# Closer due times for stores, sums and set-up transfers in a planned graph kernel, with four result buffers for six

## The chip, the cores and the metric

The kernel runs on one core of a Trainium2 chip. A core has five engines that matter here: TensorE (PE in the profile, with PEld for its weight loads), VectorE (DVE), ScalarE (ACT), GpSimd (POOL) and SyncE (SP). Each works through its own queue of instructions, and they meet through semaphores. The metric is the device time of one execution in microseconds, as the median of several runs.

## What is computed

Two graph layers over 16 graphs with 1024 nodes of 64 channels each, and a dense adjacency array of 1024 x 1024 per graph that is mostly zeros:

```python
h = jnp.maximum(_layernorm(x, axis=-1), 0.0)
x = x + _L0_gnn_ref(h, adj)          # (adj / clip(row sum, 1)) @ h
h = jnp.maximum(_layernorm(x, axis=-1), 0.0)
x = x + _L1_gnn_ref(h, adj, nodemask, W1, b1, W2, b2)

# in _L1_gnn_ref:
adj_d = _dilate_adj(adj, mask)       # drops some neighbours of nodes with more than 10
agg = _weighted_nanquantile_agg(x, adj_d > 0)   # 0.25*q25 + 0.5*q50 + 0.25*q75, per channel
out = x + agg
h = jax.nn.relu(jnp.einsum('bnc,ch->bnh', out, W1) + b1)
y = jnp.einsum('bnh,ho->bno', h, W2) + b2
```

The second layer takes, for every node and channel, three quantiles over the node's neighbours. Nodes have very different numbers of neighbours, from one to about a hundred.

## The kernel before

**Layer 0.** For each graph, SP loads eight tiles of adjacency rows. TensorE transposes them, ACT copies the transposes out of PSUM, TensorE multiplies them by the normalised features, and VectorE divides by the row sums. ACT and VectorE also make a short list of the neighbours of every node: ACT takes the sign of the row (`sg`), and VectorE picks the largest keys of four segments (`rec`). The streams `loads`, `beginnings`, `signs`, `listing`, `transposes`, `products`, `channels` and `endings` do this, each graph after graph. At the end of a graph, `endings` sorts its nodes by the length of their lists and writes their records to the DRAM table `srt` with eight indirect stores from GpSimd.

**Groups and jobs.** Four graphs form a group. When its four graphs are sorted, `group` (line 1015) reads the records back, gathers one full adjacency row per partition for the longest lists (`gat_rows`), computes which neighbours are dropped, writes marks for two of them into the table of features (`tab`), and starts ten jobs. A job takes T tiles of 128 nodes with lists of equal length. It gathers the neighbours' features with one indirect DMA per list position (`places`), sorts them on VectorE by a network of minima and maxima, weighs them (`prod`), and hands them to `layers` (line 960). There TensorE adds up the terms, transposing them (`pt`), and applies W1 and W2, with ACT between; ACT writes the result `y`; VectorE adds the residual, `y + S`; and GpSimd stores the rows with one indirect DMA per tile (`out_dram`). Four more jobs with the longest lists of all, one tile each, come from `long_lists` (line 1133): their names begin with l (`lat`, `lplaces`). The 44 jobs need 124 stores and 659 gathers.

**The plan.** What sets the order of all this is the class `Plan` (line 233). It runs while the program is built. Every stream is a generator, and each `yield` names the engine that its next step needs and a function for the time at which the step may begin. The plan keeps a clock for each engine and, for each tile, the time at which it is ready, both from fixed costs per operation. Again and again it takes the step that can begin first (of equals, the one with the lower rank), and emits its instructions. On the chip there are no clocks and no due times any more: there is an order of instructions on each engine, and the waits on semaphores that the data need. A step that the plan put too close behind its operand therefore waits at the head of its engine's queue.

Three constants are added to due times for this: `LOOSE` (line 214), 15 us, between a job's last product and TensorE's terms (line 963) and between `y` and the sum (line 1005); `ROWS` (line 215), 7 us, ahead of the sort stores (line 774), of the gather of full rows (`gat_rows`, line 1036, and `lat`, line 1154) and of the marks (line 1110); and `LATE` (line 216), 25 us, between the sum and the stores (line 1010). Since results live long in this way, there are six buffers for `y` (lines 963 and 964). `SLACK`, 2 us, serves in the same way for shorter hand-overs and stays.

Of the kernel before, what the change touches and what calls it, by code (L numbers as in the profile page):

```python
# [9 lines left out]
F32 = mybir.dt.float32  # L10
# [8 lines left out]
P = 128  # L19
# [190 lines left out]
INF = float("inf")  # L210
BREATH = 0.8
AHEAD = 8
SLACK = 2.0
LOOSE = 15.0
ROWS = 7.0
LATE = 25.0


class Timed:
# [13 lines left out]
class Plan:  # L233
# [24 lines left out]
    def room(self, name, bufs):  # L258

        tiles = self.slots.get(name, ())  # L260
        if len(tiles) < bufs:
            return 0.0
        old = tiles[-bufs]
        return INF if self.users[old] else max(self.used.get(old, 0.0), self.ready.get(old, 0.0))

    def at(self, *tiles):
        return max(self.ready.get(t.tensor.name, INF) for t in tiles)
# [98 lines left out]
def list_path(ctx, tc, x, adj, nodemask, w1, b1, w2, b2, out, go):  # L366
# [3 lines left out]
    CO = w2.shape[1]  # L370
# [19 lines left out]
    mlp = ctx.enter_context(tc.tile_pool(name="mlp", bufs=2))  # L390
# [88 lines left out]
    new, free, room, at = plan.tile, plan.release, plan.room, plan.at  # L479
# [235 lines left out]
    def endings(pool, now):  # L715

        for b, st in enumerate(batch):
            now[0] = b
            g, gb = divmod(b, GB)
            yield "ACT", lambda: known(st, "rec", "row") if st["listed"] == NT else INF  # L720
            rec, total, row = st["rec"], st["total"], st["row"]

            for t in range(NT):
                nc.scalar.activation(
                    row[:, t, R0:R0 + 8 * NSEG], rec[:, t, :], AF.Relu, bias=before[:, t:t + 1]
                )


            yield "DVE", always
            found = new(pool, [P, NT, 8 * NSEG], BF, "found", 1)  # L730
            nc.vector.tensor_scalar(found, rec, 0.0, None, op0=OP.is_gt)
            d = new(tiny, [P, NT], F32, "d", 2)
            nc.vector.tensor_reduce(d, found, AX.X, OP.add)
            full = new(tiny, [P, NT], F32, "full", 2)
            nc.vector.tensor_reduce(
                full, found.rearrange("p t (s e) -> p t s e", e=8)[:, :, :, 7], AX.X, OP.max
            )
            nc.vector.scalar_tensor_tensor(d, full, float(STEPS[0]), d, op0=OP.mult, op1=OP.max)
            nc.vector.tensor_scalar(d, d, float(STEPS[0]), None, op0=OP.min)
            for s in STEPS[1:]:  # L740
                nc.vector.scalar_tensor_tensor(d, total, float(s), d, op0=OP.is_gt, op1=OP.add)
            free(rec)
            free(total)
            hot = new(tiny, [P, CLS, NT], BF, "hot", 2)
            nc.vector.tensor_tensor(
                hot, cls, d.unsqueeze(1).to_broadcast([P, CLS, NT]), OP.is_equal
            )
            yield "PE", lambda: max(at(hot), room("ps_small", 3))
            pc = new(ps_s, [P, HALF], F32, "ps_small", 3, users=1)
            K = CLS * NT  # L750
            flat = hot.rearrange("p c t -> p (c t)")
            nc.tensor.matmul(pc[:, :K], earlier, flat, start=True, stop=True)
            nc.tensor.matmul(pc[:, K:2 * K], ones, flat, start=True, stop=True)
            yield "DVE", lambda: at(pc) + SLACK
            base = new(tiny, [P, K], F32, "base", 2)
            nc.vector.tensor_tensor_scan(
                base, pc[:, K:2 * K], zeros[:, :K], 0.0, op0=OP.add, op1=OP.add
            )
            nc.vector.tensor_tensor(base, base, pc[:, K:2 * K], OP.subtract)
            nc.vector.tensor_tensor(base, base, pc[:, :K], OP.add)  # L760
            free(pc)
            nc.vector.tensor_tensor(base, base, flat, OP.mult)
            pos = new(tiny, [P, NT], F32, "pos", 2)
            nc.vector.tensor_reduce(pos, base.rearrange("p (c t) -> p t c", t=NT), AX.X, OP.add)
            low = new(tiny, [P, NT], I32, "low", 2)
            nc.vector.tensor_copy(low, pos)
            nc.vector.tensor_scalar(low, low, LSUB - 1, None, op0=OP.bitwise_and)
            nc.vector.tensor_scalar(
                pos, pos, float(GB), float(LSUB * gb), op0=OP.mult, op1=OP.add
            )  # L770
            to = new(pool, [P, NT], I32, "to", 2)
            nc.vector.scalar_tensor_tensor(to, low, float(1 - GB), pos, op0=OP.mult, op1=OP.add)
            for t in range(NT):
                yield "POOL", lambda: max(at(to), at(row)) + ROWS if "normed" in st else INF
                scatter(srt[g], row[:, t, :], to[:, t:t + 1], sorts[g])
            free(row)
            progress["batches"] = b + 1
# [21 lines left out]
    class Job:  # L799
# [160 lines left out]
        def layers(self, terms, sources):  # L960

            T, R = self.T, terms[0][0].shape[1]
            yield "PE", lambda: max(at(*sources) + LOOSE, room("y", 6), room("pt", 2))
            y = new(mlp, [P, T, CO], F32, "y", 6, users=1)
            for t0 in range(0, T, 4):
                ts = range(t0, min(t0 + 4, T))
                M = len(ts) * P
                if t0:
                    yield "PE", lambda: room("pt", 2)
                pt = new(ps_t, [P, HALF], F32, "pt", 2, users=1)  # L970
                for i, t in enumerate(ts):
                    for k, term in enumerate(terms[t]):
                        nc.tensor.matmul(
                            pt[:term.shape[1], i * P:(i + 1) * P], term, ident,
                            start=(k == 0), stop=(k == len(terms[t]) - 1),
                        )
                if t0 + 4 >= T:
                    for tile_ in sources:
                        free(tile_)
                yield "ACT", lambda: max(at(pt) + SLACK, room("ot", 2))  # L980
                ot = new(mlp, [2 * C, HALF], F32, "ot", 2)
                nc.scalar.copy(ot[:R, :M], pt[:R, :M])
                free(pt)
                yield "PE", lambda: max(at(ot) + SLACK, room("ps_small", 3))
                ph = new(ps_s, [P, HALF], F32, "ps_small", 3, users=1)
                nc.tensor.matmul(ph[:, :M], w1_sb[:R, :], ot[:R, :M], start=True, stop=True)
                yield "ACT", lambda: max(at(ph) + SLACK, room("hid", 2))
                hid = new(mlp, [H, HALF], F32, "hid", 2)
                nc.scalar.activation(hid[:, :M], ph[:, :M], AF.Relu, bias=b1_sb)
                free(ph)  # L990
                yield "PE", lambda: max(at(hid) + SLACK, room("ps_small", 3))
                py = new(ps_s, [P, HALF], F32, "ps_small", 3, users=1)
                pv = py[:, :len(ts) * CO].rearrange("p (t c) -> p t c", c=CO)
                for i, t in enumerate(ts):
                    nc.tensor.matmul(
                        pv[:, i, :], hid[:, i * P:(i + 1) * P], w2_sb, start=True, stop=False
                    )
                    nc.tensor.matmul(pv[:, i, :], ones_f[:1, :], b2_sb, start=False, stop=True)
                yield "ACT", lambda: at(py) + SLACK
                for i, t in enumerate(ts):  # L1000
                    nc.scalar.activation(
                        y[:, t, :], pv[:, i, :], AF.Copy, scale=self.mask[:, t:t + 1]
                    )
                free(py)
            yield "DVE", lambda: at(y) + LOOSE
            nc.vector.tensor_tensor(y, y, self.S[:, :, X1:R0], OP.add)
            if self.short:
                free(self.S)
            for t in range(T):
                yield "POOL", lambda: at(y) + LATE  # L1010
                scatter(out_rows, y[:, t, :], self.nodes_i[:, t:t + 1], scatters)
            free(y)
            progress["jobs"][self.g] += 1

    def group(g):
# [17 lines left out]
        )  # L1033
        nodes_i = new(grp, [P, NTAU], I32, "nodes_i", 2)
        nc.vector.tensor_copy(nodes_i, nodes)
        yield "POOL", lambda: at(nodes_i) + ROWS
        full = new(grp, [P, N], F32, "gat_rows", 1)
        gather(full, adj_rows, nodes_i[:, 0:1])
        yield "DVE", always
# [65 lines left out]
        for e in range(2):  # L1105
# [1 line left out]
                nb, cum, skip[:, e, :], None, op0=OP.is_lt, op1=OP.add,  # L1107
                accum_out=drop[:, 0, e:e + 1],
            )
        yield "POOL", lambda: at(drop) + ROWS  # L1110
        for e in range(2):
            nc.gpsimd.indirect_dma_start(
                out=pairs[:R * TS * PW, :],
# [19 lines left out]
    def long_lists(pool):  # L1133
# [4 lines left out]
        for l, K in enumerate(LONG):  # L1138
# [12 lines left out]
            nc.vector.tensor_tensor(nodes, node, noff[:, 1:2], OP.add)  # L1151
            nodes_i = new(pool, [P, 1], I32, "lnodes_i", 4)
            nc.vector.tensor_copy(nodes_i, nodes)
            yield "POOL", lambda: max(at(nodes_i) + ROWS, room("lat", 1))
            full = new(pool, [P, N], F32, "lat", 1)
            gather(full, adj_rows, nodes_i)
            yield "DVE", lambda: at(full)
# [367 lines left out]
```

## Time and profile before

| | us |
|---|---|
| median of 3 runs | 1949.79 (1947.86 to 1966.94) |
| span of the profiled run | 1953.2 |
| VectorE busy | 1252.1 (64%) |
| GpSimd busy | 965.2 (49%) |
| TensorE busy | 818.3 (42%) |
| ScalarE busy | 607.3 (31%) |

In the page, nearly all instructions carry line 227, since the plan's recording layer issues them. So the groups are told apart by their tiles, written as out<-in. The names that matter here are `prod` (a job's last products), `pt`, `ot`, `hid` (its way through TensorE and ACT), `y`, `out_dram` (its stores), `places` and `lplaces` (gathers), `srt` (sort stores), `gat_rows`, `lat` and `tab` (set-up). "DVE y L227 <- ACT y L227" is time in which VectorE stood idle ahead of its next instruction, which writes y, until ACT had written y. Layer 0 ends at about 1080 us; after that only the last group's jobs and the long lists remain.

### The profile page before, as it was taken

What the parts mean: (1) busy time and instruction counts of PE and PEld (TensorE: products, weight loads), DVE (VectorE), ACT (ScalarE), POOL (GpSimd) and SP (SyncE); (2) the same over time, 40 slices, a digit from 0 to 9 for tenths busy, and PEclk for the clock granted to TensorE, in tenths of its full rate; (3) what the DMA queues carried; (4) which work ended last, traced back from release to release, by engine and by line L of the source; (5) the groups of instructions that cost most, each with busy time, mean ns of one, the idle gap of its engine ahead of it and who ended that gap; (6) DMA issues with size and microseconds to landing.
All of it is one profiled execution on the core that took longest, in us unless ns stands there. A gap on an engine that the chain in (4) does not pass through costs nothing.

```text
span 1953.2 us, 15147 instructions
## 1 busy us (share of the span) xinstructions
PE 818.3 (42%) x3336; PEld 518.3 (27%) x3336; DVE 1252.1 (64%) x4090; ACT 607.3 (31%) x1874; POOL 965.2 (49%) x1140
## 2 busy tenths in 40 slices
PE   6778651345688236611577001000001458142155
PEld 3334421223355013410245000000001237132134
DVE  7766877636676557954642396747935779785290
ACT  7888744225465435513333000000000011010011
POOL 0123255534434654347525625478775546747723
PEclk8978875667788678755777555555555557555556
DMA  4545633213344323422201201111111101111100
GB/s 159 160 123 167 182 103 83 64 47 75 93 123 126 91 77 117 105 74 60 56 23 37 56 19 32 30 40 22 24 27 36 25 17 25 25 43 32 24 7 14
DMA packets 119013, 129.09 MB, mean 66 GB/s; under 512 B 68306, under 2 KB 86866, under 8 KB 118914
## 3 DMA queue, kind: packets, MB, share of 16 engines
q1 hardware_dynamic: 86178, 86.58, 15.6%
q0 software_dynamic: 32736, 41.47, 9.4%
q14 instruction: 71, 0.58, 0.1%
q8 instruction: 28, 0.46, 0.1%
HBM read 108.70 MB, written 19.28 MB: 66 GB/s over the span
## 4 chain that ended last, share of the span: by engine, by line
DVE 34%; PE 16%; issue 15%; another core or an unknown queue 14%; ACT 9%; POOL 8%; DMA 2%; SPq 0%; DVEq 0%; POOLq 0%; ACTq 0%
PE ps_small L227 9%; PE pt L227 7%; DVE other L227 5%; DVE places L227 5%; DVE rec L227 4%; POOL lplaces L227 3%; POOL places L227 2%; DVE lplaces L227 2%; DVE long_other L227 2%; ACT ln_sq L227 2%; ACT sg L227 2%; DVE sg L227 2%; POOL out_dram L227 2%; ACT att L227 2%
## 5 line engine op out<-in xcount | busy, mean ns | idle before, releaser
L227 POOL DMA_INDIRECT places<-tab,idx x496 | 493.1, 994 | 263.6 <-issue 141.7
L227 PE MATMUL pt<-ident,prod 128*128 128x128 f32 (+1 forms) x736 | 155.7, 371 | 553.1 <-DVE prod L227 350.2
L227 PE MATMUL ps_small<-att,h 128*65 128x512 f32 x512 | 269.8, 677 | 63.3 <-ACT h L227 42.8
L227 PEld LDWEIGHTS pt<-ident,prod 128*128 128x128 f32 (+1 forms) x736 | 127.2, 254 | 586.0 <-issue 210.5
L227 PE MATMUL pt<-ident,at 128*128 128x128 f32 x1024 | 184.9, 329 | 170.8 <-ACT att L227 83.5
L227 POOL DMA_INDIRECT srt<-row,to x128 | 125.4, 980 | 261.0 <-ACT row L227 158.6
L227 POOL DMA_INDIRECT out_dram<-y,nodes_i x124 | 129.6, 1045 | 210.9 <-issue 72.2
L227 POOL DMA_INDIRECT lplaces<-tab,lidx x163 | 172.3, 1057 | 73.0 <-issue 47.8
L227 PEld LDWEIGHTS pt<-ident,at 128*128 128x128 f32 x1024 | 139.6, 167 | 225.0 <-ACT att L227 106.8
L227 DVE MAX8 rec<-sg 128x8 f16<-128x256 f16 x512 | 180.2, 414 | 13.2 <-remote 5.8
L227 ACT COPY att<-pt 128x512 f32<-128x512 f32 x256 | 142.3, 583 | 130.9 <-remote 79.8
L227 ACT COPY ot<-pt 128x128 f32<-128x128 f32 (+3 forms) x56 | 22.4, 399 | 426.6 <-issue 175.3
L227 ACT ACTIVATE sg<-at 128x1024 f16<-128x1024 f32 x128 | 134.9, 1055 | 40.8 <-DVE rec L227 19.0
L227 DVE TENSOR_TENSOR sg<-sg,keyed 128x1024 f16<-128x1024 f16 x128 | 87.3, 682 | 81.0 <-ACT sg L227 80.8
L227 PEld LDWEIGHTS ps_small<-att,h 128*65 128x65 f32 x512 | 78.7, 159 | 208.8 <-issue 137.8
L227 PE MATMUL ps_small<-ot,w_sb 128*128 128x128 f32 (+3 forms) x112 | 56.9, 602 | 121.7 <-ACT ot L227 89.1
L227 DVE TENSOR_TENSOR other<-places,other 128x64 f32<-128x64 f32 (+6 forms) x204 | 69.8, 342 | 39.3 <-DVE places L227 11.6
L227 PE MATMUL ps_small<-w_sb,hid 128*128 128x64 f32 x256 | 68.6, 360 | 58.4 <-issue 43.0
L227 ACT ACTIVATE y<-ps_small,recs 128x64 f32<-128x64 f32 x124 | 31.5, 312 | 187.2 <-PE ps_small L227 66.3
L227 ACT ACTIVATE wu<-wu 128x39 f32<-128x39 f32 (+9 forms) x40 | 9.4, 235 | 249.7 <-issue 130.5
L227 DVE TENSOR_TENSOR places<-places,other 128x64 f32<-128x64 f32 (+2 forms) x208 | 62.4, 309 | 25.4 <-DVE other L227 10.2
L227 PEld LDWEIGHTS ps_small<-w_sb,hid 128*128 128x128 f32 x256 | 51.1, 246 | 87.7 <-issue 53.3
(208 smaller groups left out, 1652.2 us busy)
## 6 DMA issues: line engine op xcount, KB each, us to landing
at<-in_adj_dram SPq DMA_DIRECT2D x128, 512.0 KB
places<-tab,idx POOLq DMA_INDIRECT x496
tab<-row SPq DMA_DIRECT2D x16, 264.0 KB
xt<-in_x_dram SPq DMA_DIRECT2D x16, 256.0 KB
S<-srt SPq DMA_DIRECT2D x8, 390.0 KB
lplaces<-tab,lidx POOLq DMA_INDIRECT x163
recs<-srt SPq DMA_DIRECT2D x4, 544.0 KB
S<-srt SPq DMA_DIRECT2D x8, 260.0 KB
```

The lines of the kernel that those rows point to most:

```text
L227: ins = getattr(self._engine, op)(*args, **kwargs)
```

## The change

The three constants become one, `LOOSE`, of 7 us. TensorE's terms and the sum come due 7 us after their operands instead of 15, and the stores 7 us instead of 25. The gathers of full rows and the marks come due at once instead of after 7 us; the sort stores keep their 7 us. There are four buffers for `y` instead of six. The aim is that finished results leave early, that the set-up of groups and long lists starts as soon as its operands are there, and that less memory is held.

```diff
-LOOSE = 15.0
-ROWS = 7.0
-LATE = 25.0
+LOOSE = 7.0
...
-                yield "POOL", lambda: max(at(to), at(row)) + ROWS if "normed" in st else INF
+                yield "POOL", lambda: max(at(to), at(row)) + LOOSE if "normed" in st else INF
...
-            yield "PE", lambda: max(at(*sources) + LOOSE, room("y", 6), room("pt", 2))
-            y = new(mlp, [P, T, CO], F32, "y", 6, users=1)
+            yield "PE", lambda: max(at(*sources) + LOOSE, room("y", 4), room("pt", 2))
+            y = new(mlp, [P, T, CO], F32, "y", 4, users=1)
...
-                yield "POOL", lambda: at(y) + LATE
+                yield "POOL", lambda: at(y) + LOOSE
...
-        yield "POOL", lambda: at(nodes_i) + ROWS
+        yield "POOL", lambda: at(nodes_i)
...
-        yield "POOL", lambda: at(drop) + ROWS
+        yield "POOL", lambda: at(drop)
...
-            yield "POOL", lambda: max(at(nodes_i) + ROWS, room("lat", 1))
+            yield "POOL", lambda: max(at(nodes_i), room("lat", 1))
```

## The prediction

> **What bounds the kernel now.** I read the shares of the page first, then the busy time by stage, then the waits of each engine inside a stage, then single chains in the timeline. No engine fills the span, so the shares alone do not name a bound:
>
> ```profile
> PE 818.3 (42%) x3336; PEld 518.3 (27%) x3336; DVE 1252.1 (64%) x4090; ACT 607.3 (31%) x1874; POOL 965.2 (49%) x1140
> DVE 34%; PE 16%; issue 15%; another core or an unknown queue 14%; ACT 9%; POOL 8%; DMA 2%; SPq 0%; DVEq 0%; POOLq 0%; ACTq 0%
> ```
>
> The second line is the chain that ended last: it hops between VectorE (DVE), TensorE (PE) and waits. I cut the span where the work changes: layer 0 with the first two groups of lists (190 to 1080 us), the set-up of the last group and the long lists (1080 to 1485), and the last jobs (1485 to the end).
>
> ```profile
> 190.00:1080.00 890.00, 456.74 (x1858) 271.98 (x1856) 546.68 (x1815) 387.34 (x1189) 418.21 (x522) 0.70 0.32 85
> 1170.00:1485.00 315.00, 21.75 (x76) 17.54 (x76) 198.86 (x648) 7.15 (x24) 214.84 (x206) 0.51 0.14 29
> 1485.00:1953.00 468.00, 202.91 (x880) 158.36 (x880) 309.73 (x945) 52.66 (x166) 257.61 (x290) 0.59 0.12 25
> ```
>
> The columns after the length are PE, weight loads, DVE, ACT and POOL. From 1170 to 1485 GpSimd (POOL) is the bound: 214.8 us busy, plus 0.30 us of issue before nearly each of some 206 indirect DMAs, is 276 of 315 us, and 34 us of the rest are two waits at the head of its queue. In the last stage VectorE is the bound: 309.7 us busy, and most of what is left is its own waiting. These are the waits of DVE, then of POOL, in that stage, with the two POOL waits of the stage before it at the end:
>
> ```profile
> DVE y L227 <- ACT y L227: 52.6, 8, 18.3
> DVE w L227 <- ACT wu L227: 16.2, 2, 11.2
> ...
> POOL out_dram L227 <- DVE y L227: 62.2, 5, 26.1
> POOL places L227 <- DVE prod L227: 56.0, 6, 15.2
> ...
> POOL lat L227 <- DVE other L227: 17.4, 1, 17.4
> POOL lat L227 <- DVE lnodes_i L227: 16.7, 1, 16.7
> ```
>
> So the sum of line 1006 (`y + S`) already stops VectorE for 52.6 us because ACT has not yet written y, and the stores of line 1011 stop POOL for 62.2 us. POOL's 56.0 us at `places` says that the gathers wait for VectorE, not the reverse. How long a result takes from VectorE's last product to its sum, for a job of four tiles, is one chain of the timeline:
>
> ```profile
> 1551.82 0.68 DVE L227 TENSOR_TENSOR prod<-other,w 128x512 f32<-128x512 f32 x1
> ...
> 1552.65 7.43 PE L227 MATMUL pt<-ident,prod 128*128 128x128 f32 x24 [4.95 <-DVE prod L227]
> ...
> 1560.12 0.59 ACT L227 COPY ot<-pt 128x512 f32<-128x512 f32 x1 [11.05 <-PE pt L227]
> ...
> 1562.87 0.69 ACT L227 ACTIVATE hid<-ps_small,b_sb 128x512 f32<-128x512 f32 x1 [2.17 <-issue]
> ...
> 1568.66 0.93 ACT L227 ACTIVATE y<-ps_small,recs 128x64 f32<-128x64 f32 x4 [5.10 <-PE ps_small L227]
> ...
> 1569.62 0.43 DVE L227 TENSOR_TENSOR y<-y,S 128x256 f32<-128x256 f32 x1 [0.38 <-ACT y L227]
> ```
>
> The product ends at 1552.5, y at 1569.6: 17.1 us with nothing in the way. Read the same way, one tile takes 5.4 to 6.6 us, two 13.1, five 24.4 and 25.0, six 19.7 to 27.6 (mean of four: 24.5).
>
> **What the Trainium skill says.** "PSUM — Partial Sum Buffer", Engine vs sequencer instructions: the queues of ScalarE, VectorE and GpSimdE are strict FIFO, and matmuls start and complete in program order. The trace agrees: POOL stood 16.7 us at `lat` with `lplaces` gathers next in its queue. "DMA: Bandwidth & Descriptors", Anatomy of one DMA — SWDGE (gpsimd) path: a DMA's semaphore wait is served by the issuing sequencer, before dispatch. The trace agrees again (62.2 us of POOL ahead of stores). "Perfetto Trace Analysis", Roofline: low matmul and HBM use together mean a latency-bound kernel; here 42% and 66 GB/s.
>
> **The change, part by part.** No operation is added or removed: VectorE gets the same instructions in both programs. What moves is the place of instructions in four in-order queues, since the plan sorts them by its own clock. I counted the places in the two programs' instruction orders and turned counts into time with the mean durations that the trace has for each shape.
>
> *Sums (line 1005, 15 to 7) with TensorE's terms (line 963, 15 to 7).* A sum comes up to 16 us earlier after its product. A wait appears where the VectorE work between product and sum is less than the chain. In the last stage, tiles: work before, work after, in us: 1: 11.7, 4.4; 4: 16.2, 6.9; 4: 17.1, 9.1; 6: 23.2, 14.8; 6: 31.5, 15.9; 5: 41.6, 22.7; 1: 13.6, 3.5; 2: 14.1, 3.2; 1: 3.1, 4.3; 4: 16.6, 12.6; 4: 23.0, 8.1; 6: 11.3, 9.1; the others keep enough in both. With chains of 6, 13.1, 17.1, 24 and 25 us the shortfalls after are 1.6 + 10.2 + 8.0 + 9.2 + 8.1 + 0 (the wait before it covers it) + 2.5 + 9.9 + 1.7 + 4.5 + 9.0 + 14.9 = 80 us. Before, by the same rule, 18 us. The difference is 62 us. Behind each such sum stand the networks of the next jobs; POOL waits for these through the three `places` buffers, so little is given back. I take 50, from 25 (waits already there, such as the 16.2 us at `w`, fall inside the new ones) to 62.
>
> In layer 0 the sums now have wide margins: y lay ready over 13 us before its sum in 18 of 20 jobs. The work between falls from mostly 26 to 59 us to mostly 15 to 40. That stage runs 1.5 times as long as its VectorE work (890 us to 547 busy plus short gaps), so I stretch the work by 1.5; ten of the twenty chains as measured are then longer, by 127 us, or by 62 us if each starts 8 us earlier. TensorE's terms started 0.1 to 7.6 us after their product in 17 of 20 jobs; put 8 us earlier, they would stop TensorE for 83 us in sum, with transposes and products of layer 0 queued behind them, and ACT and VectorE waiting for those. These two sums overlap, and VectorE has 306 us of idle stretches in this stage to take them. I take 30, from 0 to 80.
>
> *Stores (line 1010, 25 to 7).* A store comes 18 us closer to its sum, 34 us closer to the product. In the last stage the stores that did not wait had 1 to 34 us in hand, so more of them stop POOL; its gathers run behind, but POOL has slack there (56.0 us of waiting for VectorE's products). Nothing, beside VectorE's waits. In the POOL-bound stage three one-tile stores had 19.1, 12.1 and 13.6 us in hand: 0 + 6 + 4 = 10 us at most. I take 5.
>
> *Set-up (lines 1036, 1110, 1154, 7 to 0).* Twelve DMAs take their place up to 7 us earlier. The last group's `gat_rows` and `tab` (25.3 and 15.1 us of waiting) have nothing ready behind them: nothing. The four `lat` gathers have `lplaces` behind them in the POOL-bound stage: 0 to 28 us, I take 10.
>
> *Sort stores (line 774)* keep their 7 us: nothing but their new neighbours. *Four y buffers* for six: a result lives some 34 us less, so the ring is not the bound: nothing. *The tail* needs the same last stores: nothing.
>
> Sum: 50 + 30 + 5 + 10 = 95. From 1949.8 that is 2045; I say 2040, as waits on several engines overlap.
>
> **The rivals.** *A, only the last stage pays:* layer 0's idle VectorE time hides all of its shifts. For it: 306 us of idle stretches. Against: TensorE and VectorE wait for each other there. 1950 + 50 = 2000. *B, one wait takes the place of another:* VectorE's 52.6 us at y and POOL's 62.2 us are replaced, not added to. For it: the work is unchanged and every order has some stalls. Against: the margins were what kept the sums free. About 1955. *C, faster:* group 2 starts its set-up 43 VectorE instructions earlier, group 3 34, the early gathers pay, and stores leave before the tail. 43 instructions at 0.49 us (890 us over 1815) are 21 us, and half of the 34 us at `lat` another 17: 1912, say 1915. For it: POOL's long waits are at set-up. Against: an earlier place does not make `lnodes_i` earlier. *D, a cascade:* nearly all shortfalls land on the path: 62 + 80 + 10 + 28 = 180, of which 160 stays: 2110.
>
> **How the numbers follow.** Forecast (2005 to 2085) 0.48, A (1970 to 2005) 0.20, B (within 1%) 0.12, C 0.08, D (above 2085) 0.12. Slower by over 1% is 0.48 + 0.20 + 0.12 = 0.80; same 0.12; faster 0.08. The range from 1965 to 2110 leaves out C, most of B and the upper part of D.
>
> **What would show it.** DVE y <- ACT y over the whole span well above its 58.4 us, above 100 in the last stage; that stage longer by some 50 us with the same busy time. PE waiting for `prod` more often before layer 0 ends. POOL waiting longer at `lat`. If the y waits stay near 58 us, the counted margins are wrong; if they rise and the time does not, B holds; if layer 0 ends later by over 80 us, D does.

## The result and the profile after

The change made the kernel slightly faster: 1943.07 us (median of 18 runs) against 1958.17 us (18 runs of before beside them), a ratio of 0.9928 with a 95% interval of 0.9902 to 0.9954. The forecast was 2040 us, and its range began at 1965. On three other chips the ratio was 0.9928 [0.9902, 0.9954], 0.9963 [0.9929, 0.9996] and 0.9962 [0.9934, 0.9990], so the gain is 0.4 to 0.7%.

One thing is needed to read the numbers. The runs fell on chips of two kinds. On four of them, the slower kind (A, of the result; B, D and E), the kernel before took 1954.5 to 1984.5 us; on two, the quicker kind (C and F), 1593.3 and 1593.9 us, with nearly the same busy times. So only ratios of one chip are compared, and traces of one kind with each other. The whole change was run on the slower kind alone. Two traces used below, of before on chip B and of `lat` alone on chip E, are of runs 2.0 and 1.5% above the fastest of their kernel there, so they serve only beside others.

Here are the engines and the chain of waits in the page of after:

```profile
PE 841.9 (43%) x3336; PEld 534.9 (28%) x3336; DVE 1254.0 (65%) x4090; ACT 609.1 (31%) x1874; POOL 973.1 (50%) x1140
...
DVE 23%; PE 20%; issue 19%; another core or an unknown queue 14%; ACT 12%; POOL 7%; DMA 4%; SPq 0%; DVEq 0%; POOLq 0%; ACTq 0%
```

Counts are those of before, and busy times are within 3%. The stages of after, in the columns used in the prediction:

```profile
190.00:1080.00 890.00, 471.44 (x1860) 282.61 (x1858) 555.51 (x1851) 391.23 (x1205) 428.09 (x532) 0.71 0.31 85
1170.00:1485.00 315.00, 19.45 (x70) 15.17 (x70) 215.41 (x702) 7.98 (x27) 196.55 (x190) 0.51 0.13 29
1485.00:1937.00 452.00, 211.61 (x866) 163.92 (x866) 309.56 (x940) 51.42 (x160) 271.01 (x297) 0.58 0.12 25
```

The last stage holds the same VectorE work as before (309.6 against 309.7 us) and is 16 us shorter, not 50 us longer. Yet the waits that the forecast rests on did come. The waits of after for DVE and then POOL in that stage, and at the end of POOL from 1080 to 1485 us:

```profile
DVE y L225 <- ACT y L225: 89.1, 11, 13.7
...
POOL out_dram L225 <- DVE y L225: 57.3, 7, 12.7
...
POOL out_dram L225 <- DVE rem L225: 25.2, 2, 13.5
POOL places L225 <- DVE prod L225: 13.9, 3, 7.5
...
POOL out_dram L225 <- DVE rem L225: 20.1, 1, 20.1
POOL lplaces L225 <- DVE lnodes_i L225: 17.7, 1, 17.7
POOL tab L225 <- DVE nb L225: 17.6, 1, 17.6
...
POOL lat L225 <- DVE lnodes_i L225: 6.6, 1, 6.6
```

VectorE stands 89.1 us ahead of its sums where it stood 52.6, over the whole span 122.0 for 58.4. What fell is elsewhere. On VectorE, which bounds that stage, the wait at `w` (16.2 us before) is gone, pauses of over 0.45 us at steps of the sorting networks fell from 34.8 to 10.7 us (the last section has more on these), and the time behind its last instruction fell from 18.4 to 13.3 us. On GpSimd, the wait for products fell from 56.0 to 13.9 us, and its waits at set-up fell too. The timeline of POOL shows the last group's set-up and the four `lat` gathers, first of before, then of after. The number in brackets is the wait ahead of the DMA and what ended it:

```profile
1090.26 0.97 POOL L227 DMA_INDIRECT lat<-in_adj_dram,lnodes_i  x1 [0.30 <-issue]
...
1137.99 0.94 POOL L227 DMA_INDIRECT gat_rows<-in_adj_dram,nodes_i  x1 [25.31 <-DVE nodes_i L227]
...
1167.99 0.99 POOL L227 DMA_INDIRECT tab<-drop,didx  x1 [15.05 <-DVE lkeys L227]
...
1182.74 0.94 POOL L227 DMA_INDIRECT lat<-in_adj_dram,lnodes_i  x1 [0.30 <-issue]
...
1228.28 0.94 POOL L227 DMA_INDIRECT lat<-in_adj_dram,lnodes_i  x1 [16.74 <-DVE lnodes_i L227]
...
1271.96 0.94 POOL L227 DMA_INDIRECT lat<-in_adj_dram,lnodes_i  x1 [17.43 <-DVE other L227]
```

```profile
1125.40 0.95 POOL L225 DMA_INDIRECT gat_rows<-in_adj_dram,nodes_i  x1 [0.30 <-issue]
1126.65 0.95 POOL L225 DMA_INDIRECT lat<-in_adj_dram,lnodes_i  x1 [0.30 <-issue]
...
1162.70 1.79 POOL L225 DMA_INDIRECT tab<-drop,didx  x1 [17.58 <-DVE nb L225]
...
1199.48 0.95 POOL L225 DMA_INDIRECT lat<-in_adj_dram,lnodes_i  x1 [0.30 <-DVE q L225]
...
1224.70 0.94 POOL L225 DMA_INDIRECT lat<-in_adj_dram,lnodes_i  x1 [3.28 <-DVE places L225]
...
1251.33 0.94 POOL L225 DMA_INDIRECT lat<-in_adj_dram,lnodes_i  x1 [6.60 <-DVE lnodes_i L225]
```

Before, a long list's gather went first, then eleven stores and six gathers; then `gat_rows` stood 25.3 us at the head of the queue, and the last two `lat` 34.2 us more. After, the group's `gat_rows` goes just ahead of the first `lat`, 24 gathers come before the second `lat` (ten of them behind the marks, so of the group's own jobs), and the waits at `gat_rows` and `lat` are 10.8 us with the short ones. The wait at `tab` stayed (17.6 for 15.1 us), and a longer one stands at the first `lplaces` (17.7 for 2.6 us). In these two traces the last find of layer 0's listing (`found`) starts at 1062 and 1096 us. From there to the last `lat` it takes 210 us before and 155 after, and from the last `lat` to the end 681 and 685 us. Of the 54 us, some is work moved ahead: VectorE's busy time in that stretch fell from 139 to 108 us, and in layer 0 it rose from 675 to 697. The later end of layer 0 is no finding by itself, since before on chip B also read 1097 us. On that chip the three stretches are 1097, 220 and 684 us before, and 1103, 157 and 705 us after: the set-up stretch is where it is shorter both times.

GpSimd's waits of over 0.45 us after that last find, summed from the traces, are 228 us before and 190 after on chip A, 247 and 212 on B. By name, on chip A: set-up and long lists (`gat_rows`, `tab`, `lat`, `lplaces`) fell from 99.9 to 48.5 us and gathers of jobs from 56.0 to 15.3, while stores rose from 62.2 to 125.8.

### The profile page after: what moved, and what is told of

Its sections match the earlier page's. It is cut to its first block, busy times and chain, and to the rows that moved or that the text cites. A ratio compares the mean times of both kernels' runs of the same rounds, so it can differ in the third digit from the quotient of the medians.

```text
span 1936.7 us, 15131 instructions
## 1 busy us (share of the span) xinstructions
PE 841.9 (43%) x3336; PEld 534.9 (28%) x3336; DVE 1254.0 (65%) x4090; ACT 609.1 (31%) x1874; POOL 973.1 (50%) x1140
## 4 chain that ended last, share of the span: by engine, by line
DVE 23%; PE 20%; issue 19%; another core or an unknown queue 14%; ACT 12%; POOL 7%; DMA 4%; SPq 0%; DVEq 0%; POOLq 0%; ACTq 0%
PE ps_small L225 12%; PE pt L225 8%; DVE other L225 3%; DVE places L225 3%; ACT sg L225 3%; DMA at<-in_adj_dram 3%; ACT ln_sq L225 3%; POOL lplaces L225 2%; DVE lplaces L225 2%; ACT att L225 2%; POOL places L225 2%; POOL out_dram L225 2%; DVE rec L225 2%; DVE long_other L225 2%
## 5 line engine op out<-in xcount | busy, mean ns | idle before, releaser
L225 PE MATMUL pt<-ident,prod 128*128 128x128 f32 (+1 forms) x736 | 162.6, 385 | 578.1 <-DVE prod L225 358.9
L225 PEld LDWEIGHTS pt<-ident,prod 128*128 128x128 f32 (+1 forms) x736 | 133.8, 267 | 613.1 <-DVE prod L225 306.1
L225 DVE TENSOR_TENSOR y<-y,S 128x64 f32<-128x64 f32 (+4 forms) x40 | 14.4, 361 | 128.9 <-ACT y L225 122.0
```

What stands on the lines that cost most here:

```text
L225: ins = getattr(self._engine, op)(*args, **kwargs)
```

## The experiments

Each kernel is the kernel before with one or more of its edits, so lines carry L227. Ratios are to before on the same chip, with their 95% interval.

### One part each, on chip C (before 1593.30 us)

**Stores due after 7 us**

```diff
-LATE = 25.0
+LATE = 7.0
```

> The kernel before with one edit: the stores come due 7 us after their sum instead of 25. Set-up theory (the gain of the change comes from the set-up transfers that come due at once): nothing here, ratio 0.997 to 1.003. Stores theory (results that leave early shorten the tail and free GpSimd at the end): ratio 0.990 to 0.996, with the tail after the last product shorter. Order theory (any new order moves the time by up to 1% either way, whatever constant caused it): anything from 0.99 to 1.01, with no tie between the waits at out_dram and the time.

Measured: 1607.30 us, 1.0085 [1.0070, 1.0100]. Stores alone cost a little.

**Terms and sums due after 7 us**

```diff
-LOOSE = 15.0
+LOOSE = 7.0
```

> The kernel before with one edit: TensorE's terms and VectorE's sums come due 7 us after their operands instead of 15. The prediction's theory: VectorE's waits for y rise from 58 us to over 100 and the time rises by 2 to 4%. Substitution theory: the waits for y rise to 100 us or more, other waits of VectorE fall by about as much, and the time stays within 0.5%. Order theory: 0.99 to 1.01 without a tie to the waits for y.

Measured: 1631.03 us, 1.0235 [1.0215, 1.0255], 38 us. The four-buffer kernel below, whose time is that of before, serves as the trace of before on this chip. Its largest waits of DVE, and then those of the kernel with closer sums:

```profile
DVE rem L227 <- DMA places<-tab,idx: 50.0, 11, 16.6
DVE y L227 <- ACT y L227: 44.0, 10, 13.6
DVE sg L227 <- ACT sg L227: 35.1, 16, 8.7
```

```profile
DVE y L227 <- ACT y L227: 95.2, 17, 11.9
DVE sg L227 <- ACT sg L227: 54.2, 19, 15.4
...
DVE rem L227 <- DMA places<-tab,idx: 14.9, 2, 14.6
```

The waits at y rise by 51 us, and those of layer 0's listing at `sg` by 19. But 35 us of waiting for gathers (`rem`, a job's first step) are gone: while VectorE stands at a sum, GpSimd catches up. I summed VectorE's pauses of over 0.45 us from the two traces: 262 us became 294. Of these 32 us, 25 lie before layer 0's end, 12 after the last `lat`, and between the two it is 5 us less.

**Set-up at once**

```diff
-        yield "POOL", lambda: at(nodes_i) + ROWS
+        yield "POOL", lambda: at(nodes_i)
...
-        yield "POOL", lambda: at(drop) + ROWS
+        yield "POOL", lambda: at(drop)
...
-            yield "POOL", lambda: max(at(nodes_i) + ROWS, room("lat", 1))
+            yield "POOL", lambda: max(at(nodes_i), room("lat", 1))
```

> The kernel before with one edit: the gathers of full rows and the marks come due at once instead of after 7 us (the sort stores keep their 7 us). Set-up theory: the whole gain of the change or more, ratio 0.985 to 0.994, with the last group's set-up (gat_rows) issued some 20 us earlier than 1138 us. Substitution theory: within 0.5%. The prediction's term for it: slower by 0.5%, with longer waits at lat.

Measured: 1557.10 us, 0.9770 [0.9753, 0.9787], 36 us faster. These are GpSimd's waits in the four-buffer kernel from 870 to 1317 us, and then in this kernel from 870 to 1295 us (the 31st of the 40 group jobs begins at the end of each window):

```profile
POOL tab L227 <- DVE lkeys L227: 15.0, 1, 15.0
POOL lat L227 <- DVE other L227: 13.8, 1, 13.8
POOL lat L227 <- DVE lnodes_i L227: 5.7, 1, 5.7
...
POOL gat_rows L227 <- DVE nodes_i L227: 4.1, 1, 4.1
```

```profile
POOL out_dram L227 <- DVE y L227: 4.6, 1, 4.6
POOL lat L227 <- DVE lnodes_i L227: 4.6, 1, 4.6
POOL lplaces L227 <- DVE lnodes L227: 4.2, 1, 4.2
...
POOL lat L227 <- DVE w L227: 3.9, 1, 3.9
```

The wait at `tab` is that of chip A (15.1 us there); those at `lat` and `gat_rows` are shorter than there (17.4, 16.7 and 25.3 us). `tab` waited for `lkeys`, a step of the long lists, which the plan had put ahead of the group's marks. After layer 0's end GpSimd is the bound on this chip. In the four-buffer kernel that stretch is 767 us: 543.0 busy, 144.7 of short gaps before instructions, 72.0 of waits over 0.45 us, and 7.7 us after its last store is issued. With set-up at once it is 726 us: 538.1, 143.3, 36.5 and 8.2. The waits are 35.5 us less, and the time is 36 us less. At the end the waits of DVE say the same: from 1317 us on, the four-buffer kernel has

```profile
DVE rem L227 <- DMA places<-tab,idx: 24.4, 5, 16.6
```

and the kernel with set-up at once has no such line after 1295 us: the gathers of the last jobs are there in time.

The group's set-up did not go out earlier, though it was expected to by some 20 us: `gat_rows` is issued at 919 us in this kernel and at 897 in the four-buffer one. What changed is what stands between. Here are GpSimd's set-up and first long lists in this kernel, and then in the kernel with the stores alone at 7 us:

```profile
918.72 0.96 POOL L227 DMA_INDIRECT gat_rows<-in_adj_dram,nodes_i  x1 [0.30 <-DMA S<-srt]
919.98 0.94 POOL L227 DMA_INDIRECT lat<-in_adj_dram,lnodes_i  x1 [0.30 <-issue]
...
973.60 0.94 POOL L227 DMA_INDIRECT lat<-in_adj_dram,lnodes_i  x1 [4.58 <-DVE lnodes_i L227]
974.84 1.66 POOL L227 DMA_INDIRECT lplaces<-tab,lidx  x1 [0.30 <-issue]
```

```profile
920.77 0.94 POOL L227 DMA_INDIRECT gat_rows<-in_adj_dram,nodes_i  x1 [0.30 <-DVE other L227]
922.02 0.99 POOL L227 DMA_INDIRECT lat<-in_adj_dram,lnodes_i  x1 [0.30 <-issue]
...
977.02 0.97 POOL L227 DMA_INDIRECT lplaces<-tab,lidx  x1 [28.05 <-DVE lnodes_i L227]
```

Both send `gat_rows` just ahead of the first `lat` and wait little there, although in the second the set-up keeps its 7 us. But with set-up at once, 18 gathers of the group's jobs stand between the marks and the second `lat`; with early stores there is none, GpSimd stands 28.1 us at the first `lplaces`, and layer 0 ends at 871 us for 828. So a short wait at `gat_rows` and `lat` is not the gain by itself.

**Four y buffers**

```diff
-            yield "PE", lambda: max(at(*sources) + LOOSE, room("y", 6), room("pt", 2))
-            y = new(mlp, [P, T, CO], F32, "y", 6, users=1)
+            yield "PE", lambda: max(at(*sources) + LOOSE, room("y", 4), room("pt", 2))
+            y = new(mlp, [P, T, CO], F32, "y", 4, users=1)
```

> The kernel before with one edit: four buffers for y instead of six, with the long due times kept, so that results live long in few buffers. If the buffers matter: slower by 0.3 to 1%. If not: within 0.3%. The order changes in only a few places on GpSimd and TensorE, so this also tells how far two nearly equal orders differ.

Measured: 1592.23 us, 0.9991 [0.9978, 1.0004]: nothing, as forecast.

### On chips of the first kind

**Before once more** (chip B, one profile)

> The kernel before once more, for a profile beside the parts that were run alone, where its median was 1593 us and not the 1950 to 1958 us of the first measurements. Supply theory (in the first measurements the engines stood idle where no semaphore explains it, as if their instructions came late; later runs are free of that): busy times equal within 1%, idle ahead of VectorE, ScalarE and TensorE with releaser 'remote' or 'issue' gone, no stretches in which VectorE starts an instruction every 1.40 us. Other theory (a slower TensorE clock then): the granted clock differs and the idle stays with known releasers. If this run takes 1950 us again, neither is told apart.

Measured: 2002.51 us in that run, so the two theories aren't told apart. TensorE's mean granted clock was 0.641, against 0.687 in the four-buffer kernel's trace. The waits at set-up stand at the same places as on chip A (`gat_rows` 25.8 us for 25.3 there, the last two `lat` 45.0 for 34.2).

**The whole change once more** (chip B, before 1984.50 us)

> The changed kernel once more, against the kernel before on the same chip. If it runs at 1593 us before: the parts alone multiply to 1.0085 x 1.0235 x 0.977 x 0.999 = 1.0074, so independent parts give 1.004 to 1.011. If the set-up gain is what lasts and the other parts share their waits: 0.985 to 0.998. The prediction's theory, carried over: 1.03 or more. If the run is at 1950 us again: 0.990 to 0.996.

Measured: 1968.08 us, 0.9928 [0.9902, 0.9954].

**TensorE's terms alone, and VectorE's sums alone, at 7 us** (chip B)

```diff
-            yield "PE", lambda: max(at(*sources) + LOOSE, room("y", 6), room("pt", 2))
+            yield "PE", lambda: max(at(*sources) + 7.0, room("y", 6), room("pt", 2))
```

> The kernel before with one edit: TensorE's terms come due 7 us after the last product instead of 15; the sums keep their 15. The prediction's step for layer 0 (TensorE stands ahead of a term while transposes and products queue behind): slower by 0.5 to 2%, and layer 0 ends later. If the sums carry the cost of 2.35% that both together had: within 0.5%.

> The kernel before with one edit: VectorE's sums come due 7 us after y instead of 15; the terms keep their 15. The prediction's step for the last stage (the chain from product to sum is longer than the VectorE work between): slower by 1 to 2.5%, with VectorE's waits for y above those of the kernel before by about the difference in time. If the terms carry the cost: within 0.5%.

For the sums the same edit is made at line 1005. Measured: terms 1971.54 us, 0.9947 [0.9920, 0.9974]; sums 1974.87 us, 0.9922 [0.9892, 0.9953]. Neither costs anything alone, although the sums alone bring VectorE's pauses ahead of sums to 174 us, whatever ended them, where before has 81 on this chip. So the sum of the y waits isn't a price by itself, and neither range given for the sums was met.

**The whole change and set-up at once, side by side** (chip D, before 1954.53 us)

> The changed kernel against the kernel before. So far two chips have run the pair's parts: one where the kernel before takes 1950 to 2000 us (ratio of the changed kernel 0.993 there, twice) and one where it takes 1593 us (terms and sums alone 1.0235, stores alone 1.0085, set-up alone 0.977, buffers alone 0.999). On the quick chip, independent parts give 1.0074 (1.004 to 1.011); if the set-up gain outlasts the rest, 0.985 to 0.998; the prediction's size, 1.03 or more. On the slow chip: 0.990 to 0.996 again.

> The kernel before with the set-up transfers due at once (gat_rows, lat, the marks), and nothing else changed. On the quick chip: 0.975 to 0.979 as before. On the slow chip, set-up theory: at least the whole gain of the change, ratio 0.975 to 0.992. Order theory: no tie between the two chips, anything from 0.99 to 1.01.

Measured: the whole change 1944.15 us, 0.9963 [0.9929, 0.9996]; set-up alone 1928.64 us, 0.9878 [0.9839, 0.9918]. Set-up alone beats both kernels. Its trace has 31 gathers between the first `lat` and the second, as on chip C, where before on chip A has 17.

**The change, the two moves together, and the set-up in two halves** (chip E, before 1957.67 us)

> The changed kernel again. Theory (the parts add up, and their sizes depend on the chip): on a chip where the kernel before takes about 1593 us, the parts measured there (stores 1.0085, terms and sums 1.0235, set-up 0.977, buffers 0.9991) multiply to 1.0074, so about 1605 us, slower by 0.7%; on a chip where before takes 1950 to 1990 us, 0.990 to 0.997 as in the three comparisons so far. Rival (the parts meet, and closer sums cost nothing once the set-up is early): 0.975 to 0.985 on the quick chip as well.

> TensorE's terms and VectorE's sums due after 7 us instead of 15, all else as before. If the chip is one on which before takes 1593 us: 1.0235 again. If it is one with 1950 to 1990 us: theory (the two moves alone gave 0.995 and 0.992 there, so the waits fall into time that is idle in any case) 0.985 to 1.0. Rival (terms and sums cost only when both are early, as the chain from product to result is then not covered at all) 1.01 to 1.025, or 20 to 45 us.

> Only the four gathers of full rows for the long lists (lat) due at once; group set-up keeps its 7 us. Theory (the gain of the set-up part is in the groups, whose set-up comes ahead of layer-0 work and of the long lists): 0.997 to 1.003, since nothing moves here before the last group's first jobs. Rival (the gain is the 34 us that GpSimd stood at lat): 0.98 to 0.99, with the waits at lat falling from some 34 us to under 12.

> Only the gathers of full rows and the marks of the groups (gat_rows, tab) due at once; lat keeps its 7 us. Theory: most of the set-up part's gain, 0.978 to 0.986 on a quick chip and 0.985 to 0.992 on a slow one, with waits at gat_rows and lat both shorter since the last group's set-up no longer stands behind the long lists. Rival (the gain is the waits at lat): 0.995 to 1.003.

`lat` alone is the edit at line 1154, groups alone those at lines 1036 and 1110. Measured: the change 1943.38 us, 0.9962 [0.9934, 0.9990]; terms and sums together 2008.32 us, 1.0263 [1.0189, 1.0337] from five runs, 51 us; `lat` alone 1943.59 us, 0.9933 [0.9900, 0.9965]; groups alone 1938.19 us, 0.9883 [0.9842, 0.9924]. My theory that terms and sums fall into idle time on this kind of chip is wrong: together they cost the same share as on chip C. The waits of the kernel with both, over its whole span:

```profile
POOL places L227 <- DVE prod L227: 160.2, 11, 34.2
DVE y L227 <- ACT y L227: 154.0, 18, 18.7
```

Beside before on chip A, the waits at y have nearly tripled (58.4 us there), and GpSimd's waits for products have risen by 48 (112.2 there). (The two engines stand at once, so the numbers don't add.) On the set-up, the theory's range for the groups alone was met; `lat` alone gains too, more than the theory and less than the rival said. In both traces the waits at `lat` are some 16 us, against 34 in before on chip A. That this is the cause isn't shown: TensorE's terms alone have 17 us there on chip B. GpSimd's waits after layer 0 are 209 us with `lat` alone, 214 with the groups alone, 207 in the kernel with both on chip D, and 281 with closer sums.

### Pairs, on chip F (before 1593.92 us)

> Terms and sums at 7 us, and set-up at once; stores stay at 25 us, six y buffers. On chips where before takes 1950 to 1990 us these parts measured 1.0263 and 0.988. Theory 1 (early set-up takes the cost of closer sums away, by giving the engines other work to put between a product and its sum): 0.985 to 0.998. Theory 2 (the parts add, and something else compensates): 1.01 to 1.02. On a chip with 1593 us: theory 1 under 0.99, theory 2 about 1.000.

> Terms and sums at 7 us, and stores at 7 us; set-up keeps its 7 us, six y buffers. Theory 1 (the set-up is what compensates): 1.02 to 1.04. Theory 2 (early stores compensate): 0.99 to 1.005. A third reading (how the waits of each order happen to fall matters more than any single due time, so parts neither add nor cancel by rule) would give a value that neither of the two pairs explains, such as both pairs near 1.00.

> Set-up at once and stores at 7 us; terms and sums keep 15 us, six y buffers. The parts add: 0.988 times 1.0085, so 0.996 (1950 us chips), 0.985 on a chip with 1593 us. If it is under 0.985 the stores gain once the set-up is early; if over 1.0 they cost more than alone.

> Stores at 7 us alone, so far measured only on the quick chip (1.0085). Theory (a cost of few waits of GpSimd, the same in us): 1.004 to 1.01 on a chip with 1950 to 1990 us. Rival (on such a chip stores come early without cost): 0.985 to 0.998, which would be what compensates for the closer sums.

The edits are those above, in pairs, with six y buffers. Measured, beside the product of the single ratios of chip C:

| | ratio | product of the parts |
|---|---|---|
| closer sums and set-up at once | 1.0037 [1.0023, 1.0050] | 1.0000 |
| closer sums and closer stores | 1.0239 [1.0210, 1.0267] | 1.0322 |
| set-up at once and closer stores | 1.0092 [1.0064, 1.0120] | 0.9853 |
| closer stores alone | 1.0077 [1.0053, 1.0101] | 1.0085 |

Set-up at once takes 2.0% off the kernel with closer sums (1.0037 over 1.0235): it compensates, while the stores don't. That is no more than it gains alone on chip C (2.3%), so these two parts do nearly multiply on such a chip, and theory 1 (under 0.99) does not hold there. The waits of the pair with set-up, over its whole span:

```profile
DVE y L227 <- ACT y L227: 82.1, 16, 11.3
...
POOL lat L227 <- DVE lnodes_i L227: 5.8, 1, 5.8
...
POOL lat L227 <- DVE rem L227: 3.9, 1, 3.9
```

VectorE still waits 82.1 us at y; the waits at `lat` are short. So the cost of the sums is not undone, it is paid for from another account, and not at `lat` alone: GpSimd's waits after layer 0 are 92 us, more than the 72 of the four-buffer kernel, but layer 0 ends at 814 us instead of 828. The stores cost nothing beside closer sums. There the waits at `gat_rows`, `tab`, `lat` and `lplaces` sum to 13 us, the least of all traces, and the kernel is still 2.4% slower, as layer 0 ends at 901 us and GpSimd waits 66 us ahead of stores. Beside set-up at once the stores take all of its gain: the waits at `lat` are short there too (3.3 and 6.4 us), but the first `lplaces` waits 20.5 us, and layer 0's end is at 860 us instead of 832.

## Why the prediction was wrong

**The step that failed is the set-up.** It priced the transfers (twelve due times, but sixteen DMAs, as a group has two marks) by what stands behind each in the old order, and took 10 us of loss. For the last group's `gat_rows` and `tab`, with 25.3 and 15.1 us of waiting, it said "have nothing ready behind them: nothing". Set-up at once measured -36 us on chip C and -26 us on chip D (1928.64 against 1954.53), and its sign "POOL waiting longer at `lat`" came out the other way. In the old order the seven microseconds did not keep these transfers clear of late operands: the long lists had gone first, in VectorE's queue and in GpSimd's. The trace of POOL on chip C shows the exchange. The four-buffer kernel has 17 `places` gathers between the first `lat` and the second, the kernel with set-up at once has 31. The marks are done before the second `lat`, the gathers of the group's jobs come ready, and they fill the time in which VectorE prepares the next long list. That this filling, and not the shorter wait at any one transfer, is the gain rests on the account of GpSimd's waits on chip C (72.0 to 36.5 us); no run moves the gathers alone. The objection to rival C, "an earlier place does not make `lnodes_i` earlier", was true and beside the point: `lnodes_i` needs not be earlier where GpSimd has other work to do until then. (On chip C the last `lat` goes out at 1016 us in the one and 1024 in the other, but by then 281 `places` gathers have gone out in the one and 321 in the other.)

**Terms and sums: right in kind, too high by a third to a half.** Taken 50 + 30 = 80 us; the two together measured 51 us on chip E and 38 on chip C. The rule gave a warning: for before it counts 18 us of waits in the last stage, where the trace has 52.6. In the last stage of the whole change the waits at y rose by 36.5 us, where 62 were counted and "above 100 in last stage" was asked for (89.1). The term was mis-sized since waits replace each other, most of all in the last stage: on chip C, 42 us more of pauses ahead of sums from the last `lat` on became 12 us more of all of VectorE's pauses, as the gathers were then in time; "little is given back" was wrong. Layer 0 cost 25 us of pauses there, where 30 were taken.

**Stores: 5 us taken, 14 and 16 us measured alone** (chips C and F), and nothing beside closer sums. **Buffers: right.** The tail, put at nothing, became some 5 us shorter on chip A.

**The sum.** Even with measured parts, adding fails. Closer sums (+2.6%), set-up (-1.2%) and stores (+0.8%) multiply to about +2.2% on chips like E (the stores' part was measured on C and F only), while the change measured -0.4%. So set-up, stores and buffers together take 2.9% off the kernel with closer sums (0.9962 over 1.0263), where set-up alone gains 1.2%. The pairs on chip F don't explain this, as set-up takes there what it gains alone; on chips like E the pairs weren't run, so the cause stays open. As an estimate from these runs, of the 105 us between the forecast's +90 and the measured -15, the set-up is 36, the size of terms and sums 29, the stores 9 the other way, and about half lies in the adding.

**The rivals.** B ("one wait takes the place of another", about 1955) was nearest to the time, and its sign "if they rise and the time does not" is what the trace shows. C, at 0.08, had the sign and looked at the right transfers (its 17 us at `lat`), but no cost of the sums beside it. A and D are out. The forecast treated three rows of due times as independent; it had the sign of one wrong, and the independence too.

**What stays open.** Whether the whole change is faster on a chip like C or F was not run; the parts and pairs there lie between 0.977 and 1.024, and the pair that holds its largest gain and its largest cost is 0.4% slower. Why terms alone and sums alone each gain 0.5 to 0.8% on chip B and both together cost 2.6% on chip E isn't settled either. Layer 0 ended at 1027 and 1017 us in the traces of the single ones and at 1096 with both. A cause was not isolated, and the three were not on one chip.

## What to carry to other kernels

A wait at the head of an in-order queue is not free because the instructions behind it are not ready: ask whose order made its operand late, and whether the same change moves that order too. In a planned kernel, price a due time by the chain that it starts, not only by the queue that it stops: here the transfers that begin much other work were worth putting at once, and stores, which hardly anything waits for, were better left with their margin. A wait that is gone at one place may stand at the next, so sum all waits of the engine that bounds the stretch. Parts of such a change don't add, so run the pairs, and keep the one that pays: set-up at once alone is 1.2 to 2.3% faster than before.

## What the hardware showed beyond that

The same program took 1593 us on two chips and 1954 to 1985 us on four. Here is the four-buffer kernel's page on chip C, and then before on chip B:

```profile
PE 787.0 (49%) x3336; PEld 505.2 (32%) x3336; DVE 1248.8 (78%) x4090; ACT 606.1 (38%) x1874; POOL 979.5 (61%) x1139
```

```profile
PE 823.5 (41%) x3336; PEld 522.9 (26%) x3336; DVE 1253.5 (63%) x4090; ACT 606.3 (30%) x1874; POOL 962.4 (48%) x1140
```

VectorE, ACT and POOL are busy for the same time within 2%; all the difference is idle time. About two thirds of it lie in layer 0, which ends at 828 us in the one trace and at 1097 in the other (1062 on chip A). Some of it has a form that chip C doesn't show. On chip A there are stretches in which VectorE starts one small step of a sorting network every 1.40 us, as here in the timeline of before:

```profile
1103.30 0.23 DVE L227 TENSOR_TENSOR places<-other,places 128x64 f32<-128x64 f32 x1 [1.17 <-DVE other L227]
1104.71 0.23 DVE L227 TENSOR_TENSOR other<-other,places 128x64 f32<-128x64 f32 x1 [1.18 <-DVE places L227]
1106.09 0.30 DVE L227 TENSOR_TENSOR other<-places,other 128x128 f32<-128x128 f32 x1 [1.16 <-DVE other L227]
```

On chip C such steps follow each other at 0.25 us:

```profile
873.11 0.22 DVE L227 TENSOR_TENSOR places<-other,places 128x64 f32<-128x64 f32 x1
873.36 0.23 DVE L227 TENSOR_TENSOR other<-other,places 128x64 f32<-128x64 f32 x1
```

After layer 0, VectorE's pauses of over 0.45 us at network steps are 83 us in before on chip A and 105 on B, 22 to 35 us in four traces of the whole change on A, B, D and E, and none in the four-buffer kernel on C. Their fall on chip A, 58 us, is larger than the rise of the pauses ahead of sums in the same stretch, 45 us (70 to 115). So part of the gain on such chips, and of what the adding missed there, may be that the new order meets fewer of these stalls. It isn't tied to the change's parts: the kernel with closer sums alone has 59 us of them and is slower, set-up alone has 65 and is faster. What causes them no run here shows. For VectorE's idle time on these chips the profile often names no releaser (147 us on chip A before, 55 after, none in the four-buffer kernel), so its sums by releaser leave something out there.
